# Layer 3's bias tables into PSUM: a ScalarE copy over bf16 zero matmuls in place of f32 identity matmuls

## The chip, the cores and the metric

The kernel runs on one core of one Trainium2 chip. The core has five engines that each work through an own list of instructions in order: TensorE (PE, matmuls), VectorE (DVE), ScalarE (ACT), GpSimd (POOL) and SyncE (SP, which here only issues DMAs). They wait for each other through semaphores. The metric is the device time of one execution in microseconds (us), as the median of several runs.

## The reference

Four layers act on an input of 4 images of 64 x 64 tokens with 128 channels. Layer 0 is a selective scan in four directions with an MLP, layer 1 a full attention over the 4096 tokens of an image, layer 2 a small convolution network, layer 3 a neighbourhood attention with 4 heads and a 7 x 7 window, and an MLP. Only a part of layer 3 is touched. Its core:

```python
attn = jnp.einsum('nhijc,nhiajbc->nhijab', q, kwin)
bias = rpb[:, rel_i][..., rel_j]
attn = attn + bias[None]
attn = jax.nn.softmax(attn.reshape(B, nh, H, W, k * k), axis=-1)
out = jnp.einsum('nhijab,nhiajbc->nhijc', attn, vwin)
x = x + out @ proj_w + proj_b
```

The work beside it is the recurrence of layer 0, for 4 directions, 256 channels and 16 states at each of 4096 steps:

```python
h = jnp.exp(d_t[..., None] * A) * h + (d_t * x_t)[..., None] * B_t[:, :, None, :]
y = jnp.einsum('bkdn,bkn->bkd', h, C_t)
```

## The kernel before, in words

**The two streams.** The scan of an image (`selective_scan`) is a stream of units. A unit takes 128 rows of channel and state pairs over 2 x 512 steps: GpSimd forms `dB = du * b_rows` (L501, 128x1024), ScalarE forms two `dA = exp(A * dt)` in PSUM (L507, 128x512 each), VectorE runs two scans (L509), and the product with `c_rows` is made by GpSimd for 7 units of 16 (L522) and by VectorE for the others (L514). TensorE sums the states into `py` (L555). ScalarE also copies the last state (L516, L518). There are 512 units and 1024 `dA` for each image.

The other stream is `rest`, which takes an image whose scan is done through `scan_output` (the end of layer 0, and layer 3's MLP of the image before), `layer1`, `layer2` and `layer3_attention`. `network` writes down the scan of image k+1 first and then `rest` of image k, so that the rest of images 0, 1 and 2 runs beside the scan of images 1, 2 and 3. The rest of image 3 has no scan beside it, waits for image 3's scan, and works in a wide form (`wide`, four heads at a time) that doesn't use the lines changed here.

**What sets the order.** The kernel is written in a tile framework. Its scheduler takes all instructions with their dependences, priorities and buffers, and fixes one order for each engine before anything runs. On the chip each engine keeps to that order: an instruction whose operands are late holds all that stand behind it on its engine, whichever stream they belong to.

**Layer 3's attention, narrow form.** An image has 8 chunks `c` of 512 queries. `make_chunk(c)` loads 512 tokens, normalizes them and makes queries, keys and values. For each chunk there are 4 groups `i` of key tiles and 2 pairs `p` of heads, so 8 pairs a chunk and 64 an image. For each pair `scores` does the following: it takes a buffer `ps` of two PSUM banks (128 x 2 x 512, tag `ps`, of which there is one), puts the bias table of this kind, group and pair into it, adds the scores by matmuls of contraction 32 (L1321), and ScalarE takes the exponential into `e` (L1327). `products` then multiplies `e` with the values and with ones (L1337) into `po` and `den`; in the text this comes one group later. `finish` divides, projects and stores the chunk. The table lies in SBUF: `table` loads it from DRAM by SP (L1288, 512 KB) and keeps up to 8 of them, and loads anew where the kind changes, at chunks 0, 1 and 7. It holds the bias, and a very negative number where a key is outside the window, so it must be added before the exponential.

`make_chunk` uses the same single buffer `ps` (tag `ps`) for its own matmuls, and has two buffers for the tokens `x`. The tokens of chunk c+1 can be loaded when chunk c-1 has been stored.

**The lines changed.** For each of the two heads of a pair an f32 matmul of the table with the identity writes the table into the bank and opens the accumulation (L1317). The constant `K.zeros`, one row of 512 bf16 zeros, is there already: `products` opens `po` and `den` with it (L1364).

Of the kernel before, what the change touches and what calls it, by code (L numbers as in the profile page):

```python
# [72 lines left out]
def span(c, n=LC):  # L73
    return slice(c * n, (c + 1) * n)
# [1177 lines left out]
def layer3_attention(tc, K, A, D, img, wide):  # L1252
# [5 lines left out]
    nc = tc.nc  # L1258
    NP = 4 if wide else 2
    with ExitStack() as ctx:  # L1260
# [23 lines left out]
        def table(c, i, p):  # L1284
            kind = key_kind(c)
            if (kind, i, p) not in tables:
                t = pool.tile([128, NP, LC], F32, name="table", bufs=12 if wide else 8)
                nc.sync.dma_start(t, D.biasT[kind][i][:, NP * p : NP * p + NP, :])  # L1288
                if wide:
                    nc.scalar.activation(t, t, AF.Exp)  # L1290
                tables[kind, i, p] = t
            return tables[kind, i, p]
# [20 lines left out]
        def scores(c, i, p, group):  # L1313
            ps, t = psum.tile([128, NP, LC], F32, name="pair", tag="ps"), table(c, i, p)
            if not wide:
                for u in range(NP):
                    nc.tensor.matmul(ps[:, u, :], K.ident, t[:, u, :], start=True, stop=False)  # L1317
            for n, (tile_, q0, q1, at) in enumerate(group):
                for u in range(NP):
                    head = span(NP * p + u, HD)  # L1320
                    nc.tensor.matmul(  # L1321
                        ps[:, u, at * W : (at + q1 - q0) * W],
                        ks[tile_ // 4][head, span(tile_ % 4, 128)], qs[c][head, q0 * W : q1 * W],
                        start=wide, stop=wide or n == len(group) - 1,
                    )
            e = pool.tile([128, NP, LC], F32, name="e", bufs=4)
            made = nc.scalar.activation(e, ps, AF.Exp)  # L1327
            if wide:
                made = nc.vector.tensor_mul(e, e, t)  # L1329
            return [e[:, u, :] for u in range(NP)], made  # L1330
# [55 lines left out]
        for c in range(NCH):  # L1386
            if c + 1 < NCH:
                make_chunk(c + 1)
            sums = []
            for i, group in enumerate(key_groups(c)):  # L1390
                es = []
                for p in range(4 // NP):
                    e, made = scores(c, i, p, group)
                    es += e
                    if before is not None:
                        before.pop(0)()
                for part in before or []:
                    part()
                before = products(c, i, group, es, made, sums)
# [389 lines left out]
```

## Time and profile before

| | us |
|---|---|
| median of 3 runs | 8850.11 |
| lowest and highest | 8847.51, 8874.24 |
| the profiled execution: time | 8862.31 |
| the profiled execution: span of its records | 8860.6 |

The profile belongs to one execution. Its span is 1.7 us shorter than that execution's time, and the execution is 12 us above the median. Over the span TensorE is busy for 7044.9 us, VectorE for 7139.0, ScalarE for 5689.9 and GpSimd for 7050.2; these are averages over stretches with different limits. From the start of the exponentials of each stage on ScalarE, the stretches lie as follows:

| stage of the rest | image 0 | image 1 | image 2 |
|---|---|---|---|
| layer 1's exponentials (L801) | 2544 to 3218 | 4469 to 5140 | 6374 to 7042 |
| layer 3's exponentials (L1327) | 3427 to 3990 | 5344 to 5902 | 7254 to 7786 |

The last `dA` of the last scan starts at 7650.63 us. Image 3's rest lies between 7786 and the end. A group's line in the profile gives the engine, the operation, the tile written and those read, and the count; an f32 matmul has two records in this profile, so that the 384 matmuls of L1317 stand there 768 times.

### The profile page before, as it was taken

The page shows a single profiled execution, that of the slowest core. Times are in us where ns is not written, and L with a number is a line of the kernel's source. Part 1 is how long each engine was busy: PE and PEld are TensorE (multiplying, and loading weights), DVE is VectorE, ACT ScalarE, POOL GpSimd, SP SyncE. Part 2 cuts the span into 40 slices and gives each one's busy share as a digit, 9 for nine tenths or more (in the row PEclk, how much of TensorE's full clock was granted, in tenths as well). Part 3 has the DMA queues.
Part 4 walks back from the last instruction along what each step waited for, and adds up shares of the span by engine and source line. Part 5 has one row for each costly group of instructions (what it writes and reads, how often), then busy time and mean ns, then how long its engine had stood idle before and what let it go on. Part 6 is the DMA issues. An engine that isn't in the chain of part 4 may idle for free. (4 is left out here: it accounts for less than half of the span.)

```text
span 8860.6 us, 102305 instructions
## 1 busy us (share of the span) xinstructions
PE 7044.9 (80%) x30532; PEld 2632.3 (30%) x30532; DVE 7139.0 (81%) x8531; ACT 5689.9 (64%) x11661; POOL 7050.2 (80%) x3079
## 2 busy tenths in 40 slices
PE   6835858687788888787788988777788888788987
PEld 2211313132332222233322222333322223344333
DVE  4788978787899999998899999998899999513433
ACT  5646767676676676666766676667766666454366
POOL 6888998989899999997799999998899989500000
PEclk8756868687799998887899998888899998899989
DMA  5777677777554556565454556575455565320020
GB/s 182 245 231 246 239 252 239 260 241 262 190 167 166 167 173 219 191 208 186 163 168 171 176 173 229 192 225 175 157 170 174 176 220 188 107 70 5 1 83 30
DMA packets 863923, 1576.24 MB, mean 178 GB/s; under 512 B 218597, under 2 KB 345212, under 8 KB 859645
## 3 DMA queue, kind: packets, MB, share of 16 engines
q1 hardware_dynamic: 733053, 1393.40, 47.9%
q10 hardware_dynamic: 130304, 176.19, 5.6%
q8 instruction: 245, 4.01, 0.2%
q14 instruction: 321, 2.63, 0.1%
HBM read 1276.02 MB, written 282.28 MB: 176 GB/s over the span
## 5 line engine op out<-in xcount | busy, mean ns | idle before, releaser
L501 POOL TENSOR_TENSOR dB<-du,b_rows 128x1024 f32<-128x1024 f32 x2048 | 4812.0, 2380 | 481.9 <-issue 122.5
L507 ACT ACTIVATE dA<-dt,w_A_log 128x512 f32<-128x512 f32 x4096 | 2781.4, 690 | 508.3 <-DVE hc L509 241.6
L509 DVE TENSOR_TENSOR_SCAN dA<-dA,state,dB 128x512 f32<-128x512 f32 x2128 | 2632.4, 1273 | 278.7 <-POOL dB L501 127.6
L522 POOL TENSOR_TENSOR hc<-hc,c_rows 128x1024 f32<-128x1024 f32 x832 | 1980.4, 2380 | 50.6 <-ACT state L518 22.1
L509 DVE TENSOR_TENSOR_SCAN hc<-dA,state,dB 128x512 f32<-128x512 f32 x1456 | 1802.1, 1268 | 184.6 <-ACT dA L507 106.5
L514 DVE TENSOR_TENSOR hc<-dA,c_rows 128x512 f32<-128x512 f32 x2432 | 1566.0, 677 | 81.9 <-PE py L555 66.4
L555 PE MATMUL py<-hc,pick 128*32 128x512 f32 x8192 | 1251.1, 686 | 384.9 <-POOL hc L522 282.7
L516 ACT COPY state<-dA 128x1 f32<-128x1 f32 x2128 | 327.6, 159 | 1295.4 <-DVE hc L514 1286.0
L845 PE MATMUL pa<-e,l_v 128*128 128x512 f32 x2048 | 1052.9, 645 | 24.5 <-ACT e L801 23.5
L797 PE MATMUL pair<-l_g,l_f 32*128 32x512 f32 x2048 | 527.6, 663 | 175.0 <-ACT e L801 128.0
L801 ACT ACTIVATE e<-pair 128x1024 f32<-128x1024 f32 (+1 forms) x448 | 508.4, 1135 | 225.1 <-PE pair L797 216.6
L985 POOL MEMSET l_h<- 64x128 f32 x8 | 1.8, 229 | 816.9 <-DVE l_h L959 816.9
L845 PEld LDWEIGHTS pa<-e,l_v 128*128 128x128 f32 x2048 | 372.1, 198 | 672.0 <-issue 611.0
L555 PEld LDWEIGHTS py<-hc,pick 128*32 128x32 f32 x8192 | 210.9, 116 | 1152.5 <-issue 450.9
L247 PE MATMUL ps<-band,w_conv_diag 128*128 128x504 f32 (+3 forms) x1152 | 501.0, 594 | 7.6 <-ACT delta L397 7.2
L1317 PE MATMUL pair<-table,ident 128*128 128x512 f32 x768 | 401.9, 648 | 97.0 <-ACT e L1327 74.6
L509 DVE TENSOR_TENSOR_SCAN dA<-dA,dB 128x512 f32<-128x512 f32 x304 | 356.5, 1213 | 64.6 <-POOL dB L501 54.1
L201 PE MATMUL ps<-ident,ln_xn 128*128 128x128 f32 x512 | 138.3, 368 | 316.3 <-ACT ln_xn L198 248.9
L1327 ACT ACTIVATE e<-pair 128x1024 f32<-128x1024 f32 (+1 forms) x224 | 255.0, 1138 | 202.1 <-PE pair L1321 201.6
L328 POOL TENSOR_TENSOR du<-delta,xc 128x1024 f32<-128x1024 f32 x128 | 333.5, 2612 | 57.6 <-ACT delta L397 48.9
L219 PE MATMUL ps<-xnT,w_fc_w 128*128 128x512 f32 x512 | 272.6, 667 | 61.5 <-ACT xnT L202 38.0
L247 PEld LDWEIGHTS ps<-band,w_conv_diag 128*128 128x128 f32 x1152 | 221.4, 193 | 285.7 <-issue 264.3
(275 smaller groups left out, 8628.8 us busy)
## 6 DMA issues: line engine op xcount, KB each, us to landing
b_rows<-bc_dram SPq DMA_DIRECT2D x1024, 256.0 KB
c_rows<-bc_dram SPq DMA_DIRECT2D x1024, 256.0 KB
dt<-delta_dram SPq DMA_DIRECT2D x512, 512.0 KB
du<-du_dram SPq DMA_DIRECT2D x512, 512.0 KB
delta_dram<-delta ACTq DMA_DIRECT2D x128, 512.0 KB
du_dram<-du SPq DMA_DIRECT2D x128, 512.0 KB
table<-biasT_dram SPq DMA_DIRECT2D x72, 512.0 KB
y_first_dram<-y_sum ACTq DMA_DIRECT2D x128, 256.0 KB
```

The costliest lines, as they stand in the source:

```text
L247: mm = nc.tensor.matmul(out[:, r0 - row0 : r1 - row0, c0:c1], lhsT((dy + 1) * 3 + dx + 1), src[:, r0 + dy : r1 + dy, c0 + dx : c1 + dx], s ...
L328: nc.gpsimd.tensor_mul(du.rearrange("p d (a b) -> p d a b", b=H), deltas[b].rearrange("p d (a b) -> p d a b", b=H), tk,)
L501: nc.gpsimd.tensor_mul(dB, dus[pp], mid(bt, 2))
L507: nc.scalar.activation(dA, dts[pp][:, g, :], AF.Exp, scale=S.A[:, k, j, pr, g : g + 1])
L509: nc.vector.tensor_tensor_scan(hg[:, order], dA[:, order], dB[:, g, order], 0.0 if i == 0 else state[:, j, pr, g : g + 1], ALU.mult, ALU.add,)
L514: mm = nc.vector.tensor_mul(hc[:, g, :], dA, ct)
L522: made.append(nc.gpsimd.tensor_mul(hc, hc, mid(ct, 2)))
L555: mm = nc.tensor.matmul(py[0][32 * q : 32 * q + 32, :], S.pick, hcs[q // 2][:, q % 2, :], start=(k == 1 and j == 0), stop=(j == NJS - 1),)
L797: nc.tensor.matmul(ps[:, u, :], f[quad, t // 4, span(t % 4, 128)], g[quad, c, :], start=True, stop=True)
L801: made = nc.scalar.activation(e, ps, AF.Exp)
L845: nc.tensor.matmul(pa, v[:, 8 * q + t, :], es[q], start=(t == 0 and q == 0), stop=(t == 7 and q == 3),)
L1317: nc.tensor.matmul(ps[:, u, :], K.ident, t[:, u, :], start=True, stop=False)
```

## The change

The two f32 matmuls with the identity become two bf16 matmuls of zeros with zeros, which open the accumulation in both banks. One ScalarE copy of 128 x 1024 f32 then writes the table over the zeros, and the score matmuls accumulate onto it. The copy can't start before the zero matmuls are done, and the score matmuls can't start before the copy is done. The wide form, the loads of the tables and the buffers are as they were.

```diff
             ps, t = psum.tile([128, NP, LC], F32, name="pair", tag="ps"), table(c, i, p)
             if not wide:
                 for u in range(NP):
-                    nc.tensor.matmul(ps[:, u, :], K.ident, t[:, u, :], start=True, stop=False)
+                    nc.tensor.matmul(ps[:, u, :], K.zeros[:, :128], K.zeros, start=True, stop=False)
+                nc.scalar.copy(ps, t)
             for n, (tile_, q0, q1, at) in enumerate(group):
```

One line is added, so that lines after L1317 have a number higher by one in the changed kernel: the copy is L1318, the score matmuls L1322, the exponential L1328.

## The prediction

> **What bounds the kernel now.** I read the profile from coarse to fine: first the page's busy times in forty slices, to see that the limit changes along the span; then busy times in windows cut at the stages of the rest, to find the engine that is full in each; then what that engine waited for; and last the timeline of the stretch in which layer 3 runs with no scan beside it.
>
> ```profile
> PE   6835858687788888787788988777788888788987
> DVE  4788978787899999998899999998899999513433
> ACT  5646767676676676666766676667766666454366
> POOL 6888998989899999997799999998899989500000
> ...
> 3427.35:3989.81 562.46, 456.68 (x2594) 173.22 (x2594) 528.10 (x589) 362.47 (x745) 562.46 (x244) 0.88 0.62 205
> 4049.56:4441.40 391.84, 296.26 (x1161) 146.92 (x1161) 320.20 (x455) 287.04 (x646) 308.10 (x133) 0.82 0.51 165
> 4468.50:5139.64 671.14, 602.50 (x2489) 182.58 (x2487) 634.44 (x674) 447.41 (x848) 666.75 (x288) 0.95 0.52 174
> 5343.56:5902.46 558.90, 455.86 (x2602) 170.42 (x2602) 528.16 (x593) 359.54 (x741) 558.90 (x242) 0.89 0.64 207
> 7254.45:7650.63 396.18, 312.59 (x1735) 117.80 (x1736) 371.27 (x422) 254.44 (x543) 394.01 (x170) 0.85 0.58 192
> 7650.63:7786.19 135.56, 110.95 (x670) 46.97 (x668) 8.02 (x17) 34.03 (x45) 0.00 (x0) 0.91 0.13 40
> ```
>
> The columns of a window are its length, then busy us with instruction counts for PE, weight loads, DVE, ACT and POOL, then clock and DMA. In both whole layer 3 stretches GpSimd is busy for every microsecond (562.46 of 562.46, 558.90 of 558.90), in layer 1 for 666.75 of 671.14. The view of GpSimd's waits for 3427 to 3990 has no row. So beside layers 3 and 1 the scan is bound by GpSimd, whatever the others do. The same windows restricted to L507 give 338 `dA` in 562.46 us, 404 in 671.14, 338 in 558.90 and 405 in 668.00: always 1.65 to 1.66 us for one. Only beside `scan_output` (4049 to 4441, 183 `dA` in 391.84 us) is GpSimd not full.
>
> The last window is another regime: no scan is left, GpSimd has nothing, and the remaining 24 of image 2's 64 pairs run alone. The rest of image 3 can't start before, so each microsecond of it is on the path to the end. Its pieces:
>
> ```profile
> 7687.49 1.02 ACT L1327 ACTIVATE e<-pair 128x1024 f32<-128x1024 f32 x1 [3.82 <-PE pair L1321]
> ...
> 7716.67 1.02 ACT L1327 ACTIVATE e<-pair 128x1024 f32<-128x1024 f32 x1 [4.82 <-PE pair L1321]
> 7717.75 1.98 PE L1317 MATMUL pair<-table,ident 128*128 128x512 f32 x4 [1.12 <-ACT e L1327]
> 7719.66 1.19 PE L1321 MATMUL pair<-q,k 32*128 32x448 f32 x8
> 7720.90 1.02 ACT L1327 ACTIVATE e<-pair 128x1024 f32<-128x1024 f32 x1 [3.20 <-PE pair L1321]
> ...
> L1317 PE MATMUL pair<-table,ident x768: 592/592/1222, 3423.2 to 7783.4; 128*128 128x512 f32 x192
> ...
> L1364 PE MATMUL den<-zeros x32: 371/384/629, 3387.5 to 8732.4; 1*128 1x512 bf16 x32
> ...
> L772 ACT COPY l_g<-pair 128x1024 f32<-128x1024 f32 x16 | 16.2, 1010 | 21.2 <-PE pair L771 20.8 <-ACT y_sum L572 0.4
> ```
>
> From 7716.67 to 7785.17 there are 15 pair periods, 68.5 us, so 4.57 us each: exponential, table matmuls, score matmuls, exponential, in series through the one PSUM buffer. Between 7687.49 and 7716.67, 29.2 us, the next chunk is made: the stored chunk frees the token buffer, then load, normalization, projections, all through the same buffer. A chunk alone therefore costs 29.2 + 7 x 4.57 = 61 us where a following chunk must be made, 36 us where none is.
>
> **What the Trainium skill says.** "PSUM — Partial Sum Buffer", The four PSUM rules: a ScalarE write leaves the accumulate bits alone, and a matmul without the start flag adds to it where an earlier matmul set the bit. So the zero matmuls have to stay before the copy; no run so far shows it. "ScalarE: Activation LUTs", What ACT_TABLE_LOAD costs: 186 ns + 0.833 ns an element, by estimate 1.04 us for 1024; the trace agrees (1010 for the PSUM copy L772, 1024 for L1327). "TensorE: Matmul & The Clock Gate", Single matmul latency: (398 + 512)/2.4 = 379 ns for a lone bf16 matmul; the trace has 371 to 384. "Perfetto Trace Analysis", Optimization Strategy: the most contended engine can change from regime to regime. It does here, GpSimd to 7650 and then the layer 3 chain, and the forecast is about how much of layer 3 falls into which.
>
> **The change, part by part.** Removed for each pair: four f32 records, 1.98 us on TensorE. Added: two zero matmuls, 0.6 us (an estimate: one at 0.37 and a second pipelined behind it; bounds 0.45 and 0.77), and a copy. No row copies SBUF to PSUM at this size; the nearest are 1.01 (PSUM to SBUF) and 1.02 us (the exponential). I take 1.0, with 0.9 and 1.3 as ends.
>
> Alone, a pair without products is then 0.06 + 0.6 + 0.06 + 1.0 + 0.06 + 1.24 (score matmuls until the exponential starts, 7719.66 to 7720.90) + 1.02 = 4.04 to 4.2, against 4.23 before. A pair with products: the changed built order has zero matmuls, the products (1.86 us, 7724.95 to 7726.81), score matmuls, so the copy hides beside the products: 0.06 + 0.6 + 1.86 + 1.24 + 1.02 = 4.78 against 4.84. I take 4.5 on average: the copy costs what the matmuls save. 24 pairs would give 2 us.
>
> Beside the scan, ScalarE's 192 copies add 65 us an image. It is busy for 362 of 562 us there, so there is room, but in front of GpSimd nothing is gained by a lighter TensorE. This makes the order of instructions decide. The built order of both programs can be counted. On ScalarE, from image 0's first layer 3 exponential to its last, there are 338 `dA` before and 426 after; image 1: 338 and 432. Layer 1 of image 1 has 402 and 427, of image 2 403 and 419. The `scan_output` stretches keep theirs (183 and 184, 188 and 184), as do the gaps between. So the scheduler, with more ScalarE work in layer 3, spreads each layer 3 over more of the scan. The scan is finite: image 2's layer 3 begins 239 `dA` before the last one in the old order, 12 before it in the new. At the last `dA` 40 of its 64 pairs stood behind it; now 3 do.
>
> Time of the last `dA`: the stretches at GpSimd's pace hold 338 + 402 + 338 + 403 + 239 = 1720 `dA` before and 426 + 427 + 432 + 419 + 12 = 1716 after. The slow stretches keep length and count. So it moves by -4 x 1.65 = -7 us, to 7643: longer layer 3 stretches, 88 x 1.65 = 145 us and 94 x 1.65 = 155 us, are paid by the shorter one at the end.
>
> From the last `dA` to the last exponential of image 2. Before: 7785.2 - 7650.6 = 134.5 us. After: chunk 0 has 5 pairs left, 22 us; chunks 1 to 6 each follow a made chunk, 29.2 + 7 x 4.5 = 60.7, six times 364; chunk 7 has 8 x 4.5 = 36. Sum 422, more by 287.5. What was hidden behind GpSimd, 37 pairs and five makings of a chunk, is now in the open. From there on both orders are the same, so 1075 us of image 3 (8860.6 - 7785.2) move along unchanged. The queue of SP adds nothing: a table's buffer comes free after its copy, and in the new order the eight loads of the tables of kind 1 stand ahead of chunk 0's store and wait for chunk 0's copies, but the last of these lies before that store in any case.
>
> Sum against the profiled execution: 8862 - 7 + 287 = 9142; against the median of 8850 it is 9130.
>
> **The rivals.** (a) The scan also loses its pace. A copy waits for zero matmuls that stand on TensorE behind `py` matmuls, which wait for GpSimd's products; `dA` exponentials stand behind the copy, and VectorE, busy for 94%, waits for them. If each of the 131 pairs beside the scan takes 1 us from GpSimd, it is 9260. For: ScalarE's exponentials already wait for TensorE there. Against: GpSimd had no wait at all in spite of that, and four `dB` buffers let it run ahead. (b) The making of a chunk costs less alone than the single 29.2 us gap shows, say 17: six times 12 less, 9058. For: it is one sample, in which TensorE was slow after idling (3.60 us for the first table matmuls). Against: the load must wait for the store in both orders. (c) The other side: layer 3 beside the scan is TensorE's affair (456.68 of 562 us), 64 pairs save 1.4 us each, 88 us an image, and image 2's layer 3 ends with the scan at 7650. Then 135 us fall away: 8715. It decides if the ScalarE order had fewer than 338 `dA` in a layer 3; it has 426, so it would need an order on the chip other than the built one. (d) The change does nothing to the order that counts, and the copies balance the matmuls: 8848.
>
> **How the numbers follow.** Forecast 0.70; (a) 0.14; (b) 0.12; (c) 0.02; (d) 0.02. The range takes (b) in at its low end and most of (a): the zero matmul and copy bounds give 61 pairs x 0.4 = 24 us either way, the gap six times 10, so 9040 to 9230. A measurement of this kernel tells about 0.3% from no change. Faster 0.02, same 0.01, slower 0.97, with part of (d) on either side of that bound.
>
> **What would show it.** GpSimd's busy share in layer 3 of images 0 and 1 stays at 100% with 1.65 us for a `dA`, over stretches of about 703 and 711 us; if it falls, (a). The last `dA` is near 7643, and image 2's layer 3 then runs alone for 422 us, with six gaps of 29 us between exponentials; gaps near 17 say (b). The copy takes 1.0 us, a pair alone 4.5. The part after image 2 keeps its 1075 us. I am wrong in the whole if image 2's layer 3 starts well before the scan's end.

## The result, and the profile after

| | before | after |
|---|---|---|
| median, us | 8852.27 of 4 runs | 9240.62 of 4 runs |
| lowest and highest | 8847.51, 8874.24 | 9231.28, 9243.22 |
| profiled span | 8860.6 | 9241.5 |
| TensorE's granted clock over the span | 0.860 | 0.813 |

The ratio of after to before is 1.0434, with the interval 1.0421 to 1.0447. The kernel became slower by 388 us. The forecast of 9130 had the direction, but the time lies 11 us above the top of its range.

The busy times in forty slices of the kernel after, with the row of the granted clock:

```profile
PE   6736768686798987767788887676798986688987
...
DVE  4788878788899999988899999998899990012433
ACT  5646767675666676767766677677766673345365
POOL 6988999989899989998899989998899980000000
PEclk8757878786899986678899987668899985579989
```

GpSimd (POOL) falls to 0 earlier in the row only because the same scan is followed by more. The new feature is in the two slices after it: PE shows 6 6, where all slices without a scan had 7 or more before, and the clock row shows 5 5. That is as low as in the third slice, in which PE is at 3.

The next view is busy time in windows, with the columns of the prediction's windows. The rows are layer 3 of image 0, layer 3 of image 1, the stretch from the last `dA` of the last scan to image 2's last layer 3 exponential, and what is left of image 3.

```profile
3428.18:4138.98 710.80, 508.81 (x2662) 166.00 (x2654) 662.67 (x730) 486.73 (x967) 706.85 (x306) 0.70 0.61 201
5532.47:6247.55 715.08, 523.26 (x2670) 169.08 (x2669) 673.50 (x740) 495.06 (x980) 715.08 (x310) 0.68 0.60 199
7628.39:8160.67 532.28, 349.67 (x1688) 139.77 (x1684) 20.64 (x67) 168.51 (x228) 1.66 (x1) 0.56 0.07 20
8160.67:9241.50 1080.83, 918.47 (x4502) 421.72 (x4502) 361.21 (x567) 570.50 (x862) 0.79 (x4) 0.92 0.12 38
```

The first two rows say that GpSimd is still full beside layer 3 (706.85 of 710.80, 715.08 of 715.08), and that the stretches became longer all the same, by 148 and 156 us. The third row was 135.56 us at clock 0.91 before. It is now 532.28 us at clock 0.56. The account of the span closes with it: the last `dA` comes 22.2 us earlier (7628.39 against 7650.63), the stretch after it, to the end of image 2's last exponential, is longer by 396.7 us (532.28 - 135.56), and the tail by 6.4 us (1080.8 - 1074.4). The sum is 380.9, which is 9241.5 - 8860.6.

The timeline of that third stretch, for two pairs (start, length, engine, line, what is written and read, count, and in brackets how long the engine had been idle and what released it):

```profile
7911.45 1.02 ACT L1328 ACTIVATE e<-pair 128x1024 f32<-128x1024 f32 x1 [2.35 <-PE pair L1322]
7912.52 1.01 PE L1317 MATMUL pair<-zeros 1*128 1x512 bf16 x2 [1.18 <-ACT e L1328]
...
7913.62 1.02 ACT L1318 COPY pair<-table 128x1024 f32<-128x1024 f32 x1 [1.15 <-PE pair L1317]
...
7914.69 2.19 PE L1322 MATMUL pair<-q,k 32*128 32x448 f32 x8 [1.16 <-ACT pair L1318]
...
7916.98 1.02 ACT L1328 ACTIVATE e<-pair 128x1024 f32<-128x1024 f32 x1 [2.35 <-PE pair L1322]
...
7922.30 1.13 PE L1322 MATMUL pair<-q,k 32*128 32x320 f32 x8
...
7923.54 1.02 ACT L1328 ACTIVATE e<-pair 128x1024 f32<-128x1024 f32 x1 [3.36 <-PE pair L1322]
7924.61 0.59 PE L1317 MATMUL pair<-zeros 1*128 1x512 bf16 x2 [1.18 <-ACT e L1328]
...
7926.36 2.07 PE L1322 MATMUL pair<-q,k 32*128 32x320 f32 x8 [1.16 <-ACT pair L1318]
```

The first pair, without products, takes 5.53 us from exponential to exponential; the second, with products, 6.56. TensorE now stops twice in a pair without products, for 1.18 us behind the exponential and for 1.16 us behind the copy. The score matmuls of 32 x 448 take 2.19 us; the prediction's timeline has the same eight in 1.19. The last lines show that the pace changes within microseconds: eight score matmuls of 32 x 320 take 1.13 us at 7922.30 and 2.07 at 7926.36, and the zeros between them take 0.59.

The clock of 0.56 is a mean. The records of the granted clock hold two values only, half and full, and in this stretch they alternate. Two neighbouring windows:

```profile
7921.94:7925.36 3.42, 2.08 (x30) 1.07 (x22) 0.00 (x0) 1.09 (x2) 0.00 (x0) 1.00 0.00 0
7925.36:7959.49 34.13, 24.90 (x144) 10.42 (x144) 0.00 (x0) 10.13 (x10) 0.00 (x0) 0.50 0.00 0
```

In the second the clock stays at half for 34.13 us, though TensorE is busy for 24.90 of them.

The copy takes what was forecast, and its row over all 192 pairs says so (minimum, median, maximum in ns):

```profile
L1318 ACT COPY pair<-table x192: 992/1016/1038, 3424.4 to 8156.4; 128x1024 f32<-128x1024 f32 x192
L1317 PE MATMUL pair<-zeros x384: 370/580/630, 3422.5 to 8155.7; 1*128 1x512 bf16 x192
```

So there are two effects to be told apart: more pairs of image 2 behind the end of the scan (the order), and slower pairs there (the clock).

### The profile page after: what moved, and what is told of

Read it like the earlier page. It is cut to its first block, busy times and chain, and to the rows that moved or that the text cites. A ratio compares the mean times of both kernels' runs of the same rounds, so it can differ in the third digit from the quotient of the medians.

```text
span 9241.5 us, 101846 instructions
## 1 busy us (share of the span) xinstructions
PE 7143.8 (77%) x30148; PEld 2613.2 (28%) x30148; DVE 7147.6 (77%) x8531; ACT 5876.2 (64%) x11853; POOL 7045.0 (76%) x3079
## 5 line engine op out<-in xcount | busy, mean ns | idle before, releaser
L555 PE MATMUL py<-hc,pick 128*32 128x512 f32 x8192 | 1329.3, 724 | 412.3 <-POOL hc L522 318.2
L1322 PE MATMUL pair<-q,k 32*128 32x64 f32 (+4 forms) x1920 | 376.4, 561 | 117.5 <-ACT pair L1318 111.0
L1328 ACT ACTIVATE e<-pair 128x1024 f32<-128x1024 f32 (+1 forms) x224 | 254.7, 1137 | 244.6 <-PE pair L1322 244.1
L1351 DVE TENSOR_TENSOR oT<-rec,po 128x512 f32<-128x512 f32 x32 | 21.8, 681 | 486.4 <-ACT rec L1349 485.0
```

Of the source, the lines that this page charges most:

```text
L555: mm = nc.tensor.matmul(py[0][32 * q : 32 * q + 32, :], S.pick, hcs[q // 2][:, q % 2, :], start=(k == 1 and j == 0), stop=(j == NJS - 1),)
L1322: nc.tensor.matmul(ps[:, u, at * W : (at + q1 - q0) * W], ks[tile_ // 4][head, span(tile_ % 4, 128)], qs[c][head, q0 * W : q1 * W], start= ...
```

## The experiments

Each kernel was compared with the kernel before, run beside it on the same chip. Lines in the fences are those of the kernel named, so a copy or a score matmul can have a number a few higher than above. "Alone" is the stretch from the last `dA` to image 2's last layer 3 exponential, and counts of `dA` within a layer 3 are those of the built order, as in the prediction.

**Order and clock apart: copies in images 0 and 1 alone.** The theory: the longer layer 3 stretches of images 0 and 1 set how many pairs of image 2 are left; the clock sets how long they take. If image 2 keeps its identity matmuls, the first stays and the second goes.

```diff
                 for u in range(NP):
-                    nc.tensor.matmul(ps[:, u, :], K.zeros[:, :128], K.zeros, start=True, stop=False)
-                nc.scalar.copy(ps, t)
+                    if img < 2:
+                        nc.tensor.matmul(ps[:, u, :], K.zeros[:, :128], K.zeros, start=True, stop=False)
+                    else:
+                        nc.tensor.matmul(ps[:, u, :], K.ident, t[:, u, :], start=True, stop=False)
+                if img < 2:
+                    nc.scalar.copy(ps, t)
```

> The changed kernel, but image 2's layer 3 gets its tables by identity matmuls. Its built order is the changed one up to there: the last dA near 7628, 61 pairs left. If the changed way of bringing the table makes image 2's layer 3 slow by TensorE's clock, its stretch alone goes at a clock of 0.9, 4.57 us a pair and 29.2 us for making a chunk, 422 us, and the time is 9241 - 110 = 9130. If layer 3 alone is slow whatever brings the table, the clock stays at 0.56 and the time at 9240.

Measured: 9133.07 us, ratio 1.0325 (1.0308 to 1.0342). The window of its stretch alone:

```profile
7624.00:8051.78 427.78, 316.73 (x1810) 136.47 (x1806) 20.64 (x67) 106.60 (x167) 2.35 (x2) 0.86 0.08 25
```

The last `dA` is where it was after the change (7624.00), and as much of image 2 is left, but the clock is 0.86 and the stretch is 104.5 us shorter than the 532.3 with copies. The medians differ by as much: 9240.62 - 9133.07 = 107.6. So 286 us of the loss come with the copies of images 0 and 1, as later work in the open; that is the prediction's step (280 us) without a disturbed clock. The other 108 us belong to image 2's own pairs.

**The other half: copies in image 2 alone.** The same edit with the condition turned round (`img == 2`).

> Copies in image 2's layer 3 only. The built order is that of before until image 2's layer 3, which begins 239 dA before the last one, and leaves 29 pairs after it. At the low clock (6.2 us a pair, 31.7 for making a chunk, two of them) these take 231 us instead of 134.5: 8950. If the clock is high there, 27 x 4.5 + 2 x 29.2 = 180: 8897.

Measured: 8950.47 us, ratio 1.0116 (1.0099 to 1.0133). The window of its stretch alone:

```profile
7638.02:7870.86 232.84, 159.48 (x798) 62.85 (x797) 9.61 (x26) 75.57 (x97) 1.75 (x1) 0.58 0.08 26
```

29 pairs are left (24 before), and the clock is down at 0.58 as soon as pairs with copies run with no scan beside them. The effect of the clock doesn't need the changed order of the images before.

**Is it the load on ScalarE that spreads layer 3?** The prediction gave this as the reason for the new order. Here the kernel before gets the same copy, but into a spare SBUF buffer that nobody reads: the load is there, the chain of the pair is as before.

```diff
                 for u in range(NP):
                     nc.tensor.matmul(ps[:, u, :], K.ident, t[:, u, :], start=True, stop=False)
+                spare = pool.tile([128, NP, LC], F32, name="spare", bufs=1)
+                nc.scalar.copy(spare, t)
```

> The kernel before, with one ScalarE copy more for each of the 192 pairs: the table goes to a spare buffer in SBUF that nobody reads. So it has the added ScalarE load of the change, 65 us an image, without the wait between zero matmuls and scores. If that load is what spreads layer 3 over the scan, as the prediction had it, image 2's layer 3 begins near the scan's end and the time is 9000 us or more. If it is the longer chain of each pair through the one PSUM buffer, the built order (346 dA for a layer 3, 219 left when image 2's begins, 25 pairs left at the last dA) holds: one pair more alone, 8850 to 8875.

Measured: 8931.01 us, ratio 1.0101 (1.0084 to 1.0119). The time missed its forecast. The order answers the question: 346 `dA` in image 0's layer 3, against 338 before and 426 after. The load alone moves 8 of 88. In the profiles, which differ by 62 us, the loss has two other parts: the last `dA` comes 31 us later than before (7682.04 against 7650.63), and the stretch alone is 27 us longer. Here are the windows of image 1's layer 3 and of the stretch alone, and a row of ScalarE's waits in the first (total us, times, longest):

```profile
5354.31:5951.99 597.68, 461.84 (x2620) 173.78 (x2620) 542.23 (x604) 415.33 (x813) 574.71 (x249) 0.87 0.60 196
7682.04:7845.02 162.98, 123.01 (x728) 53.00 (x724) 10.60 (x27) 50.26 (x71) 3.66 (x2) 0.88 0.11 37
```

```profile
ACT spare L1319 <- DMA table<-biasT_dram: 19.9, 11, 5.2
```

GpSimd is busy for 574.71 of 597.68 us in image 1's layer 3: 23 us are lost (in image 0's it is 10). ScalarE's idle copy waits 19.9 us for the loads of tables there, and the `dA` exponentials stand behind it. That this wait is what GpSimd lost is likely, but not shown. The changed kernel itself doesn't lose these, since its GpSimd stays full. The stretch alone is longer because the one pair more is the last of a chunk: with it a second making of a chunk (31.1 us between two exponentials) comes behind the end of the scan, where the expectation counted a single pair.

**Does TensorE's busy share set the clock?** If it does, filling TensorE with cheap work should raise the clock. In the changed kernel, image 2's pairs get eight zero matmuls in place of two.

```diff
-                for u in range(NP):
-                    nc.tensor.matmul(ps[:, u, :], K.zeros[:, :128], K.zeros, start=True, stop=False)
+                for n in range(8 if img == 2 else 2):
+                    nc.tensor.matmul(ps[:, n % 2, :], K.zeros[:, :128], K.zeros, start=n < 2, stop=False)
                 nc.scalar.copy(ps, t)
```

> The changed kernel with more work for TensorE: in image 2's layer 3 each of the two zero matmuls is made four times (three of them add zeros). Each pair has six bf16 matmuls more in its chain, 1.3 us at full clock and 2.6 at half. If the clock falls because TensorE has too little to do, and comes back with these, a pair alone takes about 5.8 us instead of 6.2, clock 0.8 or more, and the time falls to 9200. If the pairs are slow by their chain alone, 61 pairs get 1.3 to 2.6 us longer: 9320 to 9400.

Measured: 9392.95 us, ratio 1.0622 (1.0604 to 1.064). Here is the window of the stretch alone:

```profile
7621.76:8306.62 684.86, 501.07 (x2096) 193.32 (x2088) 18.98 (x65) 169.51 (x230) 0.76 (x1) 0.55 0.05 17
```

TensorE is busy for 73% of the stretch (501.07 of 684.86), more than the 66% of the changed kernel, and the clock stays at 0.55. The six matmuls more are simply added to each pair: eight of them take 3.57 us where the clock is at half.

**The same number of matmuls over 128 rows.** `K.zeros` gets 128 rows; image 2's eight zero matmuls use all of them, all others one row as before. The number of matmuls, their 512 columns and all waits are equal to those of the last kernel; only the contraction is longer, and the data are still zeros.

```diff
-    K.zeros = pool.tile([1, LC], mybir.dt.bfloat16, name="zeros")
+    K.zeros = pool.tile([128, LC], mybir.dt.bfloat16, name="zeros")
...
+                for n in range(8 if img == 2 else 2):
+                    zeros = K.zeros if img == 2 else K.zeros[:1, :]
+                    nc.tensor.matmul(ps[:, n % 2, :], zeros[:, :128], zeros, start=n < 2, stop=False)
```

> As e4_zeros_four, but in image 2's layer 3 the zero matmuls have 128 rows of zeros instead of one. If the number of rows at work is what the clock answers to, it goes to 0.8 or more, 5.8 us a pair: 9200 to 9220. If zeros don't count, whatever their rows, or if the clock answers to something else, it stays at 9390 as with one row.

Measured: 9244.77 us, ratio 1.0438 (1.042 to 1.0455), above its forecast. Its window of the stretch alone, and a pair of its timeline:

```profile
7626.19:8162.55 536.36, 350.14 (x2059) 152.53 (x2080) 20.66 (x67) 169.58 (x229) 1.94 (x1) 0.81 0.07 21
```

```profile
7931.21 1.89 PE L1318 MATMUL pair<-zeros 128*128 128x512 bf16 x7 [1.18 <-ACT e L1329]
...
7933.19 1.02 ACT L1319 COPY pair<-table 128x1024 f32<-128x1024 f32 x1 [2.03 <-PE pair L1318]
...
7934.26 1.13 PE L1323 MATMUL pair<-q,k 32*128 32x320 f32 x8 [1.16 <-ACT pair L1319]
```

The clock is 0.81 instead of 0.55, at a lower busy share (65%), with the two stops of a pair unchanged (1.18 and 1.16 us). The stretch is 148.5 us shorter than with one-row zeros. The score matmuls of 32 x 320 take 1.13 us here, where the changed kernel's at 7926.36 took 2.07 behind the same stop. This pair of runs shows that the clock is a cause of time by itself, that the rows in use weigh in it, and that TensorE's busy time alone doesn't set it. The extra matmuls eat the gain here; that is why the total only equals that of the changed kernel.

**Only two zero matmuls, over 128 rows, in all narrow images.** This keeps the gain and leaves out the filler: the changed kernel with a 128-row `K.zeros` for the pairs, and one row of it for `po` and `den`.

> The changed kernel, where the two zero matmuls of a pair have 128 rows of zeros instead of one; nothing else, and as many instructions. In the built order a layer 3 now takes 385 and 378 dA instead of 426 and 432, and 41 pairs are left at the last dA instead of 61. If the rows raise TensorE's clock as four times as many of them did, a pair alone takes 4.5 to 4.9 us and a making 29: five pairs' rest, four chunks of 61 and one of 36 are 284 us instead of the 134.5 of before, 9000. If two of them a pair are too few for the clock (0.56, 6.2 us a pair), 356 us: 9075.

Measured: 9015.47 us, ratio 1.0192 (1.0179 to 1.0206), 225 us faster than the change as it was made. The window of its stretch alone:

```profile
7613.63:7936.68 323.05, 195.64 (x1145) 83.46 (x1156) 15.68 (x47) 113.71 (x154) 3.63 (x2) 0.69 0.07 22
```

The clock rises to 0.69. The order moved as well: 385 `dA` in image 0's layer 3 (426 with one-row zeros), and 41 pairs left at the last `dA` in place of 61. So this run isn't a clean measure of the clock, and its time lies between its two forecasts. Most of its gain is the shorter list of pairs: at the pace of the changed kernel (31.8 us where a chunk is made, 6.2 for any other pair) its 41 pairs with four makings would take 357 us, by estimate, so some 175 of the 209 us saved in this stretch come from the list and 34 from the clock. It also gives the price of the changed pair at full clock: from 7798.39 to 7802.46 the granted clock is 1.00, and this pair, without products, takes 4.07 us.

**Shorter stops.** In the changed kernel, half of the products of image 2 were held until the zero matmuls of a chunk group's second pair, so that each copy has products beside it.

```diff
-                    nc.tensor.matmul(ps[:, u, :], K.zeros[:, :128], K.zeros, start=True, stop=False)
+                    opened[0] = nc.tensor.matmul(ps[:, u, :], K.zeros[:, :128], K.zeros, start=True, stop=False)
...
-        def product(out, tile_, q0, q1, at, values, es, made, last):
+        def product(out, tile_, q0, q1, at, values, es, made, last, hold=None):
...
+                if hold is not None:
+                    after(tc, mm, hold, mybir.DependencyClass.NoSync)
...
-                    product(*w)
+                    product(*w, hold=opened[0] if img == 2 and i < 3 else None)
```

> The changed kernel with another order on TensorE in image 2's layer 3: half of the products of a group wait for the zero matmuls of the second pair, so that each pair's copy has products beside it. TensorE's work is the same, its idle stretches are shorter. If the clock follows the idle time, it goes to 0.8 or more, a pair alone takes 4.0 to 4.2 us instead of 6.2, and the time is 9100 to 9120. If the clock stays near 0.56, a pair takes 6.0 or more and the time stays at 9210 to 9240.

Measured: 9226.22 us, ratio 1.0421 (1.0403 to 1.0438). The window of the stretch alone:

```profile
7623.64:8142.48 518.84, 353.08 (x1692) 134.17 (x1684) 20.26 (x67) 167.47 (x228) 1.47 (x1) 0.56 0.07 21
```

It is 13.4 us shorter, with the clock as low as before (0.56) at a busy share of 68%. The edit changed that share by 2 points only, so it says little on how many stops a higher clock would allow.

**Identity matmuls and the copy.** In image 2 the f32 identity matmuls stand in place of the zeros and the copy follows them: the activity of the old pair with the stops of the new one.

```diff
                 for u in range(NP):
-                    nc.tensor.matmul(ps[:, u, :], K.zeros[:, :128], K.zeros, start=True, stop=False)
+                    if img == 2:
+                        nc.tensor.matmul(ps[:, u, :], K.ident, t[:, u, :], start=True, stop=False)
+                    else:
+                        nc.tensor.matmul(ps[:, u, :], K.zeros[:, :128], K.zeros, start=True, stop=False)
                 nc.scalar.copy(ps, t)
```

> The changed kernel, but in image 2's layer 3 the identity matmuls of before stand in place of the zero matmuls, and the copy follows them as well (it writes the table over the table). More work in each pair's chain than in the changed kernel, 1.4 us at full clock. If real f32 work of 128 rows keeps the clock at 0.85 or more, a pair alone takes 5.9 us and a chunk's making 29.2: 9205 to 9220, faster than the changed kernel although it does more. If the clock stays at 0.56, the identity matmuls take 3.8 us and a pair 9: 9380 or more.

Measured: 9262.05 us, ratio 1.0453 (1.0435 to 1.047), between its two forecasts. The window of the stretch alone:

```profile
7629.79:8193.73 563.94, 381.11 (x1844) 152.99 (x1836) 20.22 (x67) 170.05 (x231) 1.34 (x1) 0.77 0.07 20
```

The clock is 0.77: the 128-row matmuls bring most of it back, but with the second stop of a pair it is lower than the 0.86 of the same matmuls without a copy. TensorE's busy share is lower too (68% against 74%), and these two runs don't tell the stops from the share.

**A shorter chain, from the other side: tables as two bf16 parts.** The kernel before with each table stored as a bf16 number and a bf16 remainder, brought by two bf16 matmuls with a bf16 identity, and no copy.

```diff
                 for u in range(NP):
-                    nc.tensor.matmul(ps[:, u, :], K.ident, t[:, u, :], start=True, stop=False)
+                    for part in range(2):
+                        nc.tensor.matmul(ps[:, u, :], K.ident16, t[:, u, part, :], start=part == 0, stop=False)
```

`make_bias` splits the tables with two more VectorE operations for each group of keys, and stores the parts too.

> The other way to a lighter TensorE, without ScalarE: each table is kept as two bf16 parts (the bf16 value and the bf16 value of the rest), and two bf16 identity matmuls a head bring it, 0.86 us a pair instead of 1.98. The chain of a pair gets shorter, and in the built order a layer 3 takes 316 and 322 dA instead of 338; 17 pairs are left at the last dA instead of 24. If the place in the order and the chain decide, image 2's layer 3 ends 30 to 50 us earlier: 8800 to 8820. If TensorE's clock falls here too (5 us a pair or more), the gain goes back: 8830 to 8850.

Measured: 8867.33 us, ratio 1.0013 (1.0007 to 1.002): no gain, and its forecast was missed. The order did follow the chain: 316 `dA` in image 0's layer 3, 17 pairs left, and 94 us alone, by this window:

```profile
7701.92:7795.96 94.04, 72.44 (x493) 31.34 (x500) 8.10 (x17) 26.84 (x38) 3.58 (x2) 0.85 0.19 58
```

But the last `dA` comes at 7701.92, 51 us later than before. The delay is there in the first scan: its middle, `dA` 513, starts at 1177.6 in place of 1119.3. The one new piece ahead of it is the splitting and storing of the parts, whose 24 VectorE operations take 57 us between 584 and 835. So what was won at the end was paid at the start, most likely for the splitting; a run with the splitting alone wasn't made.

**The shortest chain: tables in bf16 alone.** The tables are made in bf16 from the start, so no splitting is needed, and one bf16 identity matmul for each head brings them. The bias of layer 3 is thereby rounded to bf16, in the wide form too.

```diff
-        T = pool.tile([128, HEADS * NR, W], F32, name="T")
+        T = pool.tile([128, HEADS * NR, W], BF16, name="T")
...
-                bt = pool.tile([128, HEADS, RC, W], F32, name="bt")
+                bt = pool.tile([128, HEADS, RC, W], BF16, name="bt")
...
-                t = pool.tile([128, NP, LC], F32, name="table", bufs=12 if wide else 8)
+                t = pool.tile([128, NP, LC], BF16, name="table", bufs=3 if wide else 8)
...
-                    nc.scalar.activation(t, t, AF.Exp)
+                    raw, t = t, pool.tile([128, NP, LC], F32, name="factor", bufs=12)
+                    nc.scalar.activation(t, raw, AF.Exp)
...
-                    nc.tensor.matmul(ps[:, u, :], K.ident, t[:, u, :], start=True, stop=False)
+                    nc.tensor.matmul(ps[:, u, :], K.ident16, t[:, u, :], start=True, stop=False)
```

> The kernel before with the bias tables in bf16 from their making on, so that one bf16 matmul with a bf16 identity brings a head's table (0.45 us a pair instead of 1.98) and ScalarE gets nothing more; the tables are rounded to bf16. The pair's chain is shorter, and in the built order a layer 3 takes 283 to 296 dA instead of 338; image 2's ends 79 dA before the last one, so that no pair is left alone. The 134.5 us of image 2's layer 3 after the last dA go, and the clock of a stretch alone has no part left: last dA near 7650, 1075 us to 1090 us after it, 8730 to 8760. If a lower clock beside the scan made the scan late, 8800 or more.

Measured: 8690.25 us, ratio 0.9821 (0.9808 to 0.9834): faster than both kernels, and some 40 us better than the lower end of its forecast. Its windows are layer 3 of image 1, layer 3 of image 2, from its end to the last `dA`, and image 3's rest:

```profile
5152.83:5642.72 489.89, 365.60 (x2341) 136.10 (x2369) 463.78 (x524) 328.57 (x686) 489.89 (x212) 0.82 0.62 202
7003.93:7494.80 490.87, 371.68 (x2345) 139.90 (x2372) 464.18 (x525) 329.95 (x689) 489.08 (x212) 0.82 0.62 200
7494.80:7633.12 138.32, 68.91 (x270) 21.59 (x270) 134.96 (x156) 67.90 (x150) 129.53 (x57) 0.65 0.58 187
7644.00:8688.50 1044.50, 888.22 (x4406) 407.22 (x4404) 352.54 (x536) 561.23 (x832) 0.80 (x4) 0.93 0.09 28
```

GpSimd is full as ever (489.89 of 489.89), so no `dA` became cheaper: image 1's layer 3 is shorter because 294 of them are ordered into it. Image 2's layer 3 is over 138 us before the scan ends, and no pair runs alone. Against the profiled execution of before, 17.5 us come from an earlier last `dA` (7650.6 to 7633.1), 134.5 from the stretch alone, which is gone, and 20 from the tail (1075.4 to 1055.4), together 172 of 8860.6 - 8688.5. How much of it is due to the halved table loads wasn't tried.

**The order against the chain.** Built orders of six kernels, with what is in the pair's chain for the table:

| what brings the table | `dA` in image 0's layer 3 | pairs left at the last `dA` |
|---|---|---|
| one bf16 identity matmul for each head | 283 | 0 |
| two bf16 identity matmuls for each head | 316 | 17 |
| f32 identity matmuls (before) | 338 | 24 |
| the same, and an idle ScalarE copy outside the chain | 346 | 25 |
| zeros over 128 rows, then a copy | 385 | 41 |
| zeros over one row, then a copy (the change) | 426 | 61 |

In these six the count grows when operations are put into the chain through the one PSUM buffer, and load outside the chain hardly moves it. The chain isn't the whole reason: one-row zeros spread layer 3 over 41 `dA` more than 128-row zeros, with the same dependences, and why stays open. More buffers for `pair`, which would break the chain, weren't tried.

## Why the prediction was right in its direction and wrong in its time

**What bounds the scan: right.** Layer 3 beside the scan was forecast as 703 and 711 us with GpSimd full; it is 710.8 and 715.1, with GpSimd busy for 706.85 and 715.08. For a `dA` that is 710.8 / 426 = 1.67 and 715.1 / 432 = 1.66 us, against 1.65. Rival (a), a scan that loses its pace, didn't come: only 3.9 us of idle GpSimd stand in the first stretch and none in the second. The clock fell beside the scan as well (0.70 and 0.68, from 0.88 and 0.89), and cost nothing there, because TensorE doesn't bound these stretches.

**The last `dA`: right.** Forecast 7643, measured 7628.39. The 15 us between them, 0.2% of the way to there, have no named cause.

**How much of layer 3 is left: right.** 61 pairs and six makings of a chunk run after the last `dA`, as the built order said. Rival (c), layer 3 ending with the scan, was excluded by that order, and rightly. Its place turned out to exist in another kernel: tables in bf16 alone gave 8690 where (c) said 8715. Rival (d) was refuted by the 388 us.

**The price of the pairs left: the failed step.** The prediction's term was "I take 4.5 on average: the copy costs what the matmuls save", a chunk of 60.7 us and 422 us in all. Measured were 531.3, to the start of the last exponential as in the forecast (8159.65). The six gaps between exponentials where a chunk is made are 31.6 to 32.1 us, on average 31.8 in place of 29.2: together 16 us more, so rival (b), which had 17, is refuted. The other 55 periods take (531.3 - 6 x 31.8) / 55 = 6.2 us in place of 4.5: 93 us more. The sum is 109, and with the last `dA` and the tail it gives the whole miss of the span: 109.3 - 15.3 + 6.4 = 100.4, which is 9241.5 against 8860.6 - 7 + 287.5 = 9141.1.

The operations were sized rightly at full clock: the copy at 1.0 (1.016 measured), the two zero matmuls at 0.6 (0.59 at 7924.61), and a pair without products at 4.04 to 4.2 (4.07 in the kernel with two zero matmuls over 128 rows). What was missing is that the edit lowers the clock at which TensorE's whole part of the chain runs. In the pair of 5.53 us above, the zeros took 1.01 instead of 0.6, and the scores 2.29 until the exponential instead of 1.24. That is 1.46 us, and it covers the excess over the forecast of 4.04 to 4.2 for such a pair. The prediction even held the sign to look at: the first matmuls after a chunk's load took 3.60 us, "TensorE was slow after idling", and it treated them as a doubt about a gap. With the clock held by identity matmuls in image 2, the stretch was 427.8 us and the time 9133, so the rest of the sum stands. The range failed for the same reason: its ends allowed for the copy, the zeros and the gaps, not for a lower clock.

"TensorE: Matmul & The Clock Gate" in the Trainium skill, Part 1: The HAM clock gate, says that the default state is throttled and activity releases it, and A second HAM failure mode: psum-queue depth-cycling says that small idles between groups of matmuls make the clock swing. The traces agree in kind: two stops of 1.16 and 1.18 us a pair go with a clock of 0.56, and the same eight score matmuls with 2.19 us instead of 1.19. The page speaks of how busy TensorE is. Here 73% busy on one-row zeros left the clock at 0.55 and 65% on 128-row zeros gave 0.81; in this the measurement decides.

**The reason given for the order: wrong.** "The scheduler, with more ScalarE work in layer 3, spreads each layer 3 over more of the scan" doesn't hold. The same copy outside the chain gave 346 `dA`, not 426. The counts fit a longer chain through the pair's only buffer, in which the copy is a further step, but that wasn't shown apart from other differences of the built orders. The forecast wasn't harmed by it, because it used the counts and not the reason.

**The tail: right.** 1075 us forecast, 1081.9 measured from the same point (9241.5 - 8159.65).

## What to carry to other kernels

When matmuls in a serial chain are replaced by cheaper ones plus work on another engine, price the whole chain again at a lower TensorE clock: here the score matmuls took 1.8 times as long where the clock was at half, and image 2's own pairs lost 108 us. In an order that is fixed before the run, count what stands behind the end of the binding stream in the built order: here operations added to a chain through a single buffer spread layer 3 by up to 88 `dA`, and the same load outside the chain by 8. To shorten such a chain, first try to make the data cheaper to bring (tables rounded to bf16, 8690 us) before moving the work to another engine (9241 us).

## What the runs showed of the hardware beyond what was expected

- The number of rows that the matmuls use weighs in the granted clock. In image 2's stretch alone, eight zero matmuls a pair gave 0.55 over one row and 0.81 over 128 rows, though zeros were multiplied in both; the stretch took 148.5 us less.
- The clock was at half for 34.13 us on end while TensorE was busy for 24.90 of them, and full for 3.42 us just before.
- The rows aren't all: identity matmuls gave 0.86 without a copy behind them and 0.77 with one, where TensorE stops twice a pair and is busy for 68% instead of 74%.
- A ScalarE copy of 128 x 1024 f32 from SBUF to PSUM takes 1.016 us, no different from the 1.01 us of the copy from PSUM to SBUF, and score matmuls accumulate onto what it wrote where zero matmuls had opened the banks.
